# Row normalisation tile by tile in two attention sublayers, with its last step on ScalarE and the next rows turned in halves

## The chip, the cores and the metric

The kernel runs on one core of one Trainium2 chip. A core has five engines with queues of their own: TensorE (PE; its weight loads are shown as PEld), VectorE (DVE), ScalarE (ACT), GpSimd (POOL) and SyncE (SP), which issues the DMAs. They wait for each other by semaphores. The metric is the device time of one launch in microseconds; the kernel before takes 4338.36 us (median of three runs, 4335.82 to 4339.03).

## The reference

A decoder of four layers with three sublayers each, over 64 sequences of 64 tokens with 256 features, 4096 rows in all. After every sublayer the row is normalised:

```python
x = _layernorm(x + _L3_attn_ref(x, ...), axis=-1)     # tenth sublayer
x = _layernorm(x + _L3_xattn_ref(x, ctx_2048, ...), axis=-1)  # eleventh
x = _layernorm(x + _L3_ffn_ref(x, ...), axis=-1)      # twelfth
```

`_layernorm` takes the mean from the row and divides by the root of its variance plus 1e-5. The tenth is self-attention with 16 heads of 128, in which queries, keys and outputs are divided by their root mean square and a bias grows with the distance of two tokens. The eleventh attends to a context of 64 rows for each sequence, with 16 query heads and 4 key and value heads. The twelfth is a feed-forward layer with ternary weights. Both attentions are computed in 32-bit floats.

## The kernel before, in words

The 4096 rows lie in 8 groups of 512 rows; a group `X[g]` is one buffer of 128 partitions by 4 tiles by 256 features, and it stays on the chip from the first sublayer to the last. A tile is 128 rows, that is two sequences.

The tenth and eleventh sublayers run in one loop, `l3_attentions` (line 1787). A step is a group, a tile and a half `hb` of the 16 heads, so there are 64 steps for each sublayer. The loop is a software pipeline of depth four: in turn `i` of the loop, the queries and keys of step `i` are projected, step `i-1` has its queries and keys turned and its scores made, step `i-2` has its probabilities turned and its values summed, and step `i-3` has its outputs turned and projected. The 64 steps of the tenth are followed directly by those of the eleventh.

The order of the work: the loop stands in a region in which **TensorE** alone issues in the order in which the program emits its instructions. For the other engines a scheduler fixes the order when the program is built. It puts on an engine what its own reckoning takes to be ready, and among those what was emitted first. [...] A trace shows that order: the statistics of a group's tiles are all emitted with the fourth tile, yet those of the first three run right after their own additions.

Names and lines that matter below:

- `output` (lines 1977 and 2181): adds eight heads' share to the accumulator `acc`. With the second half of the heads it also makes `z[:, t]`, the sum of `acc` and `x` (lines 1991 and 2197, VectorE). With the fourth tile it calls `layernorm` (line 339) for the whole group.
- `layernorm`: `mean_rstd` (line 322) takes the statistics of each tile (lines 331 and 334, VectorE) and then calls `rsqrt` (line 300) once for the four tiles: an addition of epsilon on VectorE (line 303) and a power of -1/2 on GpSimd (line 305), on 128 by 4 numbers. Then line 342 applies mean and root to each of the four tiles, on VectorE.
- `normalized_parts` (line 350) is another form of the same, which other sublayers use: VectorE makes `nmr`, minus the mean times the root (line 361), and ScalarE applies both (line 363). In this loop it serves the ninth sublayer, whose groups are finished one ahead of the tenth (`linear.parts`, line 72): it makes xq (line 83), y (lines 94 to 96) and the normalised rows.
- `transposed` (line 314) turns a group's rows, eight transposes of 128 by 128 into two PSUM buffers, and copies each buffer to SBUF, as `xt`. In the eleventh sublayer `rows(g)` calls it at the end of the step of tile 3, `hb` 0, for the next group (line 2207), and once from the loop for group 0 (line 1853).
- `copy` (line 286) takes ScalarE and VectorE by turns, call by call (lines 290 and 292); it copies v, q, k, qT, pt, yt and xt. There are two PSUM buffers for transposes (`tr`), which qT, kT, pt, yt and xt share.
- The squares of y and of q and k are made by ScalarE at line 1884 and summed by VectorE at line 1885; the scores of the eleventh run on VectorE from line 2144 to 2151, with the exponential at 2149 on ScalarE and the division at 2152 on GpSimd.
- The twelfth sublayer's first rows are copied to SBUF by ScalarE at line 2297, and its first matmuls are at line 2306.

The buffer `z` is one of 128 by 4 by 256, used for a group at a time.

Of the kernel before, what the change touches and what calls it, by code (L numbers as in the profile page):

```python
# [10 lines left out]
F32 = mybir.dt.float32  # L11
# [3 lines left out]
AF = mybir.ActivationFunctionType  # L15
ALU = mybir.AluOpType
# [3 lines left out]
P = 128  # L20
D = 256
S = 64
TG = 4
NTOK = TG * P
# [246 lines left out]
class Decoder:  # L271
# [67 lines left out]
    def layernorm(self, out, z, eps=1e-5):  # L339
        mv, rstd = self.mean_rstd(z, TG, eps)  # L340
        for t in range(TG):
            self.nc.vector.tensor_scalar(
                out[:, t, :], z[:, t, :], mv[:, t, 0:1], rstd[:, t : t + 1], ALU.subtract, ALU.mult
            )

    def normalized(self, out, z):
        for part in self.normalized_parts(out, z):
            part()
# [1438 lines left out]
    def l3_attentions(self, ctx, linear):  # L1787

        wk = ctx.enter_context(self.tc.tile_pool(name="l3a", bufs=2, reuse_waits="tile"))
        steps = [(g, t, hb) for g in range(self.n_groups) for t in range(TG) for hb in range(2)]
        n = len(steps)
        none = lambda *a: None
        with self.tc.manual_schedule(engines={mybir.EngineType.PE}):
            one, two = self.l3_attn(wk, steps, linear), self.l3_xattn(wk, steps)
            row = [(one, i) for i in range(n)] + [(two, i) for i in range(n)]
            for i in range(2 * n + 3):
                at = lambda j: row[j] if 0 <= j < len(row) else (None, j)

                def do(stage, name, *a):
                    which, j = at(i - stage)
                    if which is not None:
                        getattr(which, name, none)(j, *a)

                turning = i == n
                do(0, "start")
                if i <= n:
                    do(2, "value")
                    do(1, "turn", 0)  # L1810
                    if not turning:
                        do(0, "query", 0)
                    do(1, "turn", 1)
                    if not turning:
                        do(0, "query", 1)
                    do(3, "outputs_turned")
                    do(0, "key", 0)
                    do(2, "turned")
                    do(1, "scores")
                    do(0, "key", 1)  # L1820
                    do(3, "output")
                    do(2, "values")
                    if turning:

                        two.load_biases()
                        do(0, "query", 0)
                        do(0, "query", 1)
                        do(0, "late")
                else:
                    do(2, "value")  # L1830
                    if i == n + 1:
                        two.load_output()
                    do(1, "turn", 0)
                    do(0, "query", 0)
                    do(1, "key_turned")
                    do(1, "turn", 1)


                    queries = i % 2 or i >= 2 * n or two.ready(i - n)
                    if not queries:  # L1840
                        do(0, "query", 1)
                    do(3, "outputs_turned")
                    do(3, "output")
                    do(1, "scores")
                    do(2, "turned")
                    if queries:
                        do(0, "query", 1)
                    if not i % 2:
                        do(0, "late")
                    do(2, "values")  # L1850
                do(0, "end")
                if i == n - 2:
                    two.rows(0)
                if i == n - 1:
                    two.load()

    def l3_attn(self, wk, steps, linear):
# [4 lines left out]
        nc = self.nc  # L1862
# [4 lines left out]
        nc.vector.tensor_scalar(both, kw, qw, 1.0 / math.sqrt(P), ALU.mult, ALU.mult)  # L1867
        half = lambda b: slice(b * S, (b + 1) * S)
        wide = lambda a, n: a.unsqueeze(2).broadcast_to([P, a.shape[1], n])
        xts, zs, state, accs = {}, {}, {}, {}  # L1870

        def projected(i, w, u, tag, bufs):
            g, t, hb = steps[i]
# [103 lines left out]
        def output(i):  # L1977
            g, t, hb = steps[i]
            yts = state.pop((i, "yt"))
            if hb == 0:  # L1980
                accs[g, t] = self.bank("acc", tag="acc", bufs=1)
            acc = accs[g, t]
            for h in range(8):
                n = 8 * hb + h
                nc.tensor.matmul(  # L1985
                    acc[:, :D], yts[h % 2][:, h // 2, :], wp[n // 8][:, (n % 8) * D : (n % 8 + 1) * D],
                    start=n == 0, stop=n == 15,
                )
            if hb == 1:
                x, z = self.X[g], zs[g]  # L1990
                nc.vector.tensor_tensor(z[:, t, :], acc[:, :D], x[:, t, :], ALU.add)
                if t == TG - 1:
                    self.layernorm(x, z)

        def start(i):
            g, t, hb = steps[i]
            if (t, hb) == (0, 0):
                if g + 1 < self.n_groups:
                    ahead[:] = linear.parts(g + 1, wk, bank)
                zs[g] = wk.tile([P, TG, D], F32, tag="z", name="z", bufs=1)  # L2000
            if g == 0 and hb == 0:
                ps = self.transpose4([self.X[0][:, t, c * P : (c + 1) * P] for c in range(2)], "xt")
                self.copy(xts[0][:, :, t * P : (t + 1) * P], ps[:, :D].rearrange("p (c n) -> p c n", c=2))

        def end(i):
# [13 lines left out]
        bias = self.distances(wk)  # L2019
        xts[0] = wk.tile([P, 2, NTOK], F32, tag="xt", name="xt")  # L2020
        return SimpleNamespace(
            start=start, value=value, turn=turn, query=query, outputs_turned=outputs_turned, key=key,
            turned=turned, scores=scores, output=output, values=values, end=end,
        )

    def l3_xattn(self, wk, steps):
# [4 lines left out]
        nc, ins = self.nc, self.ins  # L2031
# [23 lines left out]
            w.o = self.big_weight("l3x_wo")  # L2055

        half = lambda b: slice(b * S, (b + 1) * S)
        xts, zs, tiles, state, context = {}, {}, {}, {}, self.context

        def rms(x, out, name):  # L2060

# [5 lines left out]
        def ready(i):  # L2067
            return steps[i][:2] in context.tiles

        def loaded(i):  # L2070

            for k, name in enumerate("kv"):
                t = wk.tile([P, 4, P], F32, tag=name, name=name, bufs=2)
                self.load(t.rearrange("p h d -> p (h d)"), context.dram[(*steps[i][:2], k)])
                state[i, name] = t
# [105 lines left out]
        def output(i):  # L2181
            g, t, hb = steps[i]
            yts = state.pop((i, "yt"))
            if hb == 0:
                tiles[g, t, "acc"] = self.bank("acc", tag="acc", bufs=1)
            acc = tiles[g, t, "acc"]
            for h in range(8):
                n = 8 * hb + h
                nc.tensor.matmul(  # L2189
                    acc[:, :D], yts[h % 2][:, h // 2, :], w.o[n // 8][:, (n % 8) * D : (n % 8 + 1) * D],  # L2190
                    start=n == 0, stop=n == 15,
                )
            if hb == 1:
                if t == 0:
                    zs[g] = wk.tile([P, TG, D], F32, tag="z", name="z", bufs=1)
                x, z = self.X[g], zs[g]
                nc.vector.tensor_tensor(z[:, t, :], acc[:, :D], x[:, t, :], ALU.add)
                if t == TG - 1:
                    self.layernorm(x, z)

        def rows(g):
            xts[g] = self.transposed(self.X[g], wk, "xt")

        def end(i):
            g, t, hb = steps[i]
            if (t, hb) == (TG - 1, 0) and g + 1 < self.n_groups:
                rows(g + 1)
            if hb == 1 and i + 1 < len(steps) and ready(i + 1):
                loaded(i + 1)

            if len(steps) - i in (12, 8):
                ahead.extend(self.l3_prepare(len(self.l3_rows)))
            if ahead:
                ahead.pop(0)()

        ahead = []
        cs = lambda g, t: lambda c: self.CT[g][:, c, t * P : (t + 1) * P]
        return SimpleNamespace(
            load=load, load_biases=load_biases, load_output=load_output, rows=rows, turn=turn, query=query,
            late=late, ready=ready, key_turned=key_turned, turned=turned, scores=scores, output=output, values=values, end=end,  # L2220
        )

# [225 lines left out]
```

## Time and profile before

| what | value |
|---|---|
| median of three runs | 4338.36 us (4335.82 to 4339.03) |
| the profiled execution, its own time | 4343.85 us |
| its span | 4342.1 us |
| mean granted TensorE clock | 0.979 |
| tenth sublayer, about 1925 to 3195 us | 64 steps, some 20.0 us each |
| eleventh sublayer, about 3195 to 4042 us | 64 steps, some 12.6 us each after the handover |
| VectorE addition z, lines 1991 and 2197 | 64 times, 425 ns |
| VectorE statistics on z, line 331, in these two sublayers | 64 times, 427 ns |
| VectorE application, line 342, in these two sublayers | 64 times, 407 ns |
| ScalarE application, line 363, in the tenth sublayer's stretch | 28 times, 596 ns |
| GpSimd power, line 305, rstd of 128 by 4, in the tenth | 14 times, 1008 ns |
| GpSimd power, line 305, rstd of 128 by 1, in the twelfth | 64 times, 637 ns |

How to read the lines below. A line of a timeline has start and duration in microseconds, engine, line of the code, operation, what is written and read, how often it was merged, and in square brackets the idle time of the engine just before it, with what ended that. A line of waits names who waited, for whom, how long in all, how often, and the longest. PE, DVE, ACT and POOL are the engines as named above.

### The profile page before, as it was taken

What the parts mean: (1) busy time and instruction counts of PE and PEld (TensorE: products, weight loads), DVE (VectorE), ACT (ScalarE), POOL (GpSimd) and SP (SyncE); (2) the same over time, 40 slices, a digit from 0 to 9 for tenths busy, and PEclk for the clock granted to TensorE, in tenths of its full rate; (3) what the DMA queues carried; (4) which work ended last, traced back from release to release, by engine and by line L of the source; (5) the groups of instructions that cost most, each with busy time, mean ns of one, the idle gap of its engine ahead of it and who ended that gap; (6) DMA issues with size and microseconds to landing.
All of it is one profiled execution on the core that took longest, in us unless ns stands there. A gap on an engine that the chain in (4) does not pass through costs nothing. (4 is left out here: it accounts for less than half of the span.)

```text
span 4342.1 us, 74081 instructions
## 1 busy us (share of the span) xinstructions
PE 4079.0 (94%) x28788; PEld 2635.7 (61%) x28808; DVE 3092.6 (71%) x6211; ACT 2018.1 (46%) x3695; POOL 1498.3 (35%) x1529
## 2 busy tenths in 40 slices
PE   8889998989888999989999999999989999999898
PEld 5645566666665555546666666666656666666566
DVE  6844548888665687877777777777667777887676
ACT  5555535666523566544444444444432232332443
POOL 4411111332431111115555555555533444433111
PEclk9989999999999999999999999999999999999999
DMA  2200012333200000031111111111130000100000
GB/s 84 67 21 10 1 34 65 76 77 70 72 1 12 1 1 1 10 131 25 30 25 28 27 25 30 25 29 27 30 105 20 20 23 20 25 22 14 8 17 16
DMA packets 108296, 144.01 MB, mean 33 GB/s; under 512 B 15845, under 2 KB 73381, under 8 KB 106537
## 3 DMA queue, kind: packets, MB, share of 16 engines
q1 hardware_dynamic: 107944, 139.27, 12.6%
q8 instruction: 228, 3.74, 0.4%
q14 instruction: 124, 1.01, 0.1%
HBM read 70.25 MB, written 26.76 MB: 22 GB/s over the span
## 5 line engine op out<-in xcount | busy, mean ns | idle before, releaser
L305 POOL TENSOR_TENSOR hrq<-hrq,neg_half 128x4 f32<-128x4 f32 x256 | 258.5, 1010 | 573.9 <-DVE hrq L303 571.5
L305 POOL TENSOR_TENSOR rstd<-rstd,neg_half 128x4 f32<-128x4 f32 (+1 forms) x171 | 149.4, 875 | 705.5 <-DVE rstd L303 641.2
L1188 DVE TENSOR_REDUCE mc<-sq 128x2 f32<-128x512 f32 x512 | 317.3, 682 | 64.0 <-PE sk L1186 62.8
L1194 ACT ACTIVATE e<-sk 128x512 f32<-128x512 f32 x512 | 265.4, 606 | 114.0 <-PE sk L1186 111.6
L1183 PE MATMUL sq<-l1x 32*128 32x256 f32 x2048 | 277.2, 409 | 4.9 <-DVE z L1069 3.1
L1186 PE MATMUL sk<-l1x 32*128 32x256 f32 x2048 | 254.4, 394 | 0.2 <-DMA l1x<-l1x_m 0.2
L1703 PE MATMUL p<-l3a_wq,xt 128*128 128x512 f32 x512 | 242.1, 595 | 11.1 <-DVE v L292 9.9
L305 POOL TENSOR_TENSOR hrk<-hrk,neg_half 128x4 f32<-128x4 f32 x160 | 188.5, 1178 | 177.6 <-DVE hrk L303 173.0
L1703 PE MATMUL p<-l3a_wk,xt 128*128 128x512 f32 x512 | 247.4, 606 | 0.6 <-ACT q L290 0.6
L1183 PEld LDWEIGHTS sq<-l1x 32*128 32x128 f32 x2048 | 210.1, 195 | 57.8 <-issue 22.4
L1703 PE MATMUL p<-l3x_wq,xt 128*128 128x512 f32 x512 | 242.8, 597 | 0.7 <-DVE k L2087 0.7
L2189 PE MATMUL acc<-l3x_wo,yt 128*128 128x256 f32 x1024 | 239.7, 388 | 2.5 <-ACT yt L290 1.2
L1703 PE MATMUL p<-l3a_wv,xt 128*128 128x512 f32 x512 | 234.0, 599 | 0.4 <-ACT y L94 0.4
L1985 PE MATMUL acc<-l3a_wproj,yt 128*128 128x256 f32 x1024 | 232.0, 379 | 0.5 <-DVE yt L292 0.5
L1985 PEld LDWEIGHTS acc<-l3a_wproj,yt 128*128 128x128 f32 x1024 | 194.2, 190 | 53.7 <-issue 29.2
L2063 ACT ACTIVATE sq<-q 128x512 f32<-128x512 f32 x128 | 80.6, 630 | 314.0 <-DVE q L2087 306.7
L2189 PEld LDWEIGHTS acc<-l3x_wo,yt 128*128 128x128 f32 x1024 | 196.1, 195 | 36.7 <-issue 7.4
L311 PEld LDWEIGHTS qT<-ident,q 128*128 128x128 f32 x1024 | 122.1, 142 | 121.9 <-issue 79.8
L1186 PEld LDWEIGHTS sk<-l1x 32*128 32x128 f32 x2048 | 189.7, 188 | 6.9 <-issue 2.5
L311 PE MATMUL qT<-ident,q 128*128 128x128 f32 x1024 | 159.1, 278 | 26.8 <-DVE qT L292 19.6
L1969 POOL TENSOR_TENSOR hry<-hry,neg_half 128x8 f32<-128x8 f32 x64 | 106.3, 1660 | 183.3 <-DVE hry L1965 183.3
L1222 PE MATMUL ret<-e,vt 128*32 128x256 f32 x2048 | 139.2, 387 | 17.7 <-DVE mc L1188 16.9
(401 smaller groups left out, 10189.0 us busy)
## 6 DMA issues: line engine op xcount, KB each, us to landing
vs<-v SPq DMA_DIRECT2D x320, 128.0 KB
l3x_kv<-kv SPq DMA_DIRECT2D x28, 256.0 KB
x<-in_x SPq DMA_DIRECT2D x8, 512.0 KB
ct<-in_ctxT SPq DMA_DIRECT2D x8, 512.0 KB
cn<-in_ctx SPq DMA_DIRECT2D x8, 512.0 KB
l1x<-in_ctx SPq DMA_DIRECT2D x128, 32.0 KB
l1x_x<-x SPq DMA_DIRECT2D x8, 512.0 KB
l1x<-l1x_x SPq DMA_DIRECT2D x128, 32.0 KB
```

The costliest lines, as they stand in the source:

```text
L305: nc.gpsimd.tensor_tensor(out, out, self.neg_half[:, :n], ALU.pow)
L311: self.nc.tensor.transpose(ps[:, j * P : (j + 1) * P], blk, self.ident)
L1183: nc.tensor.matmul(ps[:, n, :], x_[rows, j, part], c_[rows, j, :], start=True, stop=True)
L1186: nc.tensor.matmul(ps[:, n, :], c_[rows, j, part], x_[rows, j, :], start=True, stop=True)
L1188: nc.vector.tensor_reduce(mc[new % 2][:, ra + k, 2 * j : 2 * j + 2], ps, AX.X, ALU.max, negate=True)
L1194: nc.scalar.activation(es[rb + k], ps, AF.Exp, scale=scale)
L1222: nc.tensor.matmul(ret[32 * r : 32 * r + 32, :], vt[i % 2][:, lc, 4 * r + j, :], es[r][:, lc, :], start=lc == 0, stop=lc == 1,)
L1703: self.nc.tensor.matmul(ps, lhs(c), w(c, cols), start=c == 0, stop=c == 1 and bias is None)
L1969: nc.gpsimd.tensor_tensor(r, r, self.neg_half[:, :8], ALU.pow)
L1985: nc.tensor.matmul(acc[:, :D], yts[h % 2][:, h // 2, :], wp[n // 8][:, (n % 8) * D : (n % 8 + 1) * D], start=n == 0, stop=n == 15,)
L2063: nc.scalar.activation(sq, x, AF.Square)
L2189: nc.tensor.matmul(acc[:, :D], yts[h % 2][:, h // 2, :], w.o[n // 8][:, (n % 8) * D : (n % 8 + 1) * D], start=n == 0, stop=n == 15,)
```

## The change

The function `tile_normalized` is new. It normalises one tile of 128 rows as soon as its sum is there: the addition, the statistics, the root for this tile alone, and then a function that makes `nmr` on VectorE and applies it on ScalarE, in place of line 342. Both sublayers' `output` call it for each tile and put the function on a list, and the loop runs the list after `end` of the same turn. The buffer `z` is now 128 by 256, two of them.

In the eleventh sublayer `rows` takes a half `c` of the features. The next group's rows are turned half by half: the first at the end of the step of tile 3 with `hb` 0, the second a step later. For group 0 the loop does it at two turns of the tenth sublayer in place of one. The tenth's own turning of rows is as before.

```diff
+    def tile_normalized(self, wk, x, a):
+        nc = self.nc
+        z = wk.tile([P, D], F32, tag="z", name="z", bufs=2)
+        st = self.smallp.tile([P, 6], F32, tag="bnst1", name="bnst1", bufs=4)
+        mv = self.smallp.tile([P, 2], F32, tag="bnmv1", name="bnmv1", bufs=4)
+        r, b = self.small(1, "rstd1", bufs=4), self.small(1, "nmr1", bufs=4)
+        nc.vector.tensor_tensor(z, a, x, ALU.add)
+        nc.vector.bn_stats(st, z)
+        nc.vector.bn_aggr(mv, st)
+        self.rsqrt(r, mv[:, 1:2], 1.0, 1e-5)
+
+        def apply():
+            nc.vector.scalar_tensor_tensor(b, mv[:, 0:1], -1.0, r, ALU.mult, ALU.mult)
+            nc.scalar.activation(x, z, AF.Identity, bias=b, scale=r)
+
+        return apply
...
+        self.row_ends = []
...
                 do(0, "end")
-                if i == n - 2:
-                    two.rows(0)
+                while self.row_ends:
+                    self.row_ends.pop(0)()
+                if i in (n - 3, n - 2):
+                    two.rows(0, i - n + 3)
...
             if hb == 1:
-                x, z = self.X[g], zs[g]
-                nc.vector.tensor_tensor(z[:, t, :], acc[:, :D], x[:, t, :], ALU.add)
-                if t == TG - 1:
-                    self.layernorm(x, z)
+                self.row_ends.append(self.tile_normalized(wk, self.X[g][:, t, :], acc[:, :D]))
...
-        def rows(g):
-            xts[g] = self.transposed(self.X[g], wk, "xt")
+        def rows(g, c):
+            if c == 0:
+                xts[g] = wk.tile([P, 2, NTOK], F32, tag="xt", name="xt")
+            ps = self.transpose4([self.X[g][:, t, c * P : (c + 1) * P] for t in range(TG)], "xt")
+            self.copy(xts[g][:, c, :], ps)
...
-            if (t, hb) == (TG - 1, 0) and g + 1 < self.n_groups:
-                rows(g + 1)
+            if t == TG - 1 and g + 1 < self.n_groups:
+                rows(g + 1, hb)
```

The third of these places stands for both `output` functions, which get the same edit.

More of the change, by code (lines that the diff above doesn't have):

```diff
@@ L1869, in l3_attn @@
         wide = lambda a, n: a.unsqueeze(2).broadcast_to([P, a.shape[1], n])
-        xts, zs, state, accs = {}, {}, {}, {}
+        xts, state, accs = {}, {}, {}
         def projected(i, w, u, tag, bufs):
@@ L1999, in start @@
                     ahead[:] = linear.parts(g + 1, wk, bank)
-                zs[g] = wk.tile([P, TG, D], F32, tag="z", name="z", bufs=1)
             if g == 0 and hb == 0:
@@ L2057, in l3_xattn @@
         half = lambda b: slice(b * S, (b + 1) * S)
-        xts, zs, tiles, state, context = {}, {}, {}, {}, self.context
+        xts, tiles, state, context = {}, {}, {}, self.context
         def rms(x, out, name):
@@ L2193, in output @@
             if hb == 1:
[L2194 to L2199, printed above, removed]
-        def rows(g):
-            xts[g] = self.transposed(self.X[g], wk, "xt")
+                self.row_ends.append(self.tile_normalized(wk, self.X[g][:, t, :], acc[:, :D]))
+        def rows(g, c):
[3 more added lines that the diff above has]
+            self.copy(xts[g][:, c, :], ps)
         def end(i):
             g, t, hb = steps[i]
-            if (t, hb) == (TG - 1, 0) and g + 1 < self.n_groups:
-                rows(g + 1)
+            if t == TG - 1 and g + 1 < self.n_groups:
+                rows(g + 1, hb)
             if hb == 1 and i + 1 < len(steps) and ready(i + 1):
```

## The prediction

> **What bounds the kernel now.** I read the page first, then the busy time by stretch, then TensorE's waits, then the timeline around the waits. From here on, "z+1.68" means 1.68 us after VectorE starts the addition z of a tile, so that tiles can be laid over each other.
>
> ```profile
> span 4342.1 us, 74081 instructions
> PE 4079.0 (94%) x28788; PEld 2635.7 (61%) x28808; DVE 3092.6 (71%) x6211; ACT 2018.1 (46%) x3695; POOL 1498.3 (35%) x1529
> ```
> ```profile
> core 0: us, PE busy (x) PEld busy (x) DVE busy (x) ACT busy (x) POOL busy (x), PEclk, DMA share, GB/s
> 1925.00:3195.00 1270.00, 1249.78 (x8541) 793.90 (x8542) 922.83 (x1805) 567.33 (x977) 673.18 (x584) 1.00 0.14 32
> 3260.00:4040.00 780.00, 748.10 (x5499) 518.28 (x5497) 596.39 (x1165) 232.27 (x412) 303.06 (x288) 0.99 0.08 20
> ```
>
> The first row is the tenth sublayer, the second the eleventh without the handover. TensorE is idle for 20 of 1270 us and for 32 of 780: no change of the row normalisation can be worth more than that and a little at the two ends. So the question is which of these idle microseconds end on an instruction that the change moves. TensorE's waits, one answer for each sublayer (total, times, longest):
>
> ```profile
> PE p L1703 <- DVE v L292: 9.9, 7, 1.4
> ```
> ```profile
> PE qT L311 <- DVE qT L292: 19.6, 11, 2.2
> PE qT L311 <- ACT xt L290: 6.5, 7, 1.0
> ```
>
> Seven times each: once for each group. The timeline shows the cause in the tenth sublayer, at the last tile of group 0:
>
> ```profile
> 2120.54 0.42 DVE L1991 TENSOR_TENSOR z<-acc,x 128x256 f32<-128x256 f32 x1 [0.38 <-PE acc L1985]
> 2121.67 0.17 DVE L303 TENSOR_SCALAR rstd<-bnmv 128x4 f32<-128x4 f32 x1
> 2121.92 1.01 POOL L305 TENSOR_TENSOR rstd<-rstd,neg_half 128x4 f32<-128x4 f32 x1 [0.35 <-DVE rstd L303]
> 2122.97 1.38 DVE L342 TENSOR_SCALAR x<-z,bnmv,rstd 128x256 f32<-128x256 f32 x4 [1.12 <-POOL rstd L305]
> 2124.26 0.68 DVE L1885 TENSOR_REDUCE hry<-sq 128x4 f32<-128x512 f32 x1
> 2127.06 0.68 DVE L292 COPY v<-p 128x512 f32<-128x512 f32 x1
> 2127.79 1.98 PE L1703 MATMUL p<-l3a_wq,xt 128*128 128x512 f32 x4 [1.41 <-DVE v L292]
> ```
>
> VectorE waits 1.12 us for GpSimd's power, then applies four tiles; L1885 starts at z+3.73, in the other tiles at z+1.68. The copy of v ends late and TensorE waits 1.41. In the eleventh sublayer the same block stands in front of the score chain:
>
> ```profile
> 3344.67 0.71 DVE L303 TENSOR_SCALAR rstd<-bnmv 128x4 f32<-128x4 f32 x1
> 3346.28 1.01 POOL L305 TENSOR_TENSOR rstd<-rstd,neg_half 128x4 f32<-128x4 f32 x1
> 3347.33 1.38 DVE L342 TENSOR_SCALAR x<-z,bnmv,rstd 128x256 f32<-128x256 f32 x4 [1.36 <-POOL rstd L305]
> 3348.63 0.68 DVE L2145 TENSOR_TENSOR s<-s,mask 128x512 f32<-128x512 f32 x1
> 3352.95 0.66 PE L311 MATMUL qT<-ident,q 128*128 128x128 f32 x4 [2.23 <-DVE qT L292]
> ```
>
> L2145 starts at z+5.10, elsewhere at z+1.89; the copy of qT is late and TensorE waits 2.23, in each of seven groups. The 0.9 us on xt is the turning of the next rows: eight transposes take both PSUM buffers, and the qT transposes behind them wait for a copy.
>
> **What the Trainium skill says.** "SBUF — State Buffer", Who interferes with whom: a VectorE tensor_scalar in a two-port mode and a GpSimd instruction exclude each other for the whole instruction. The trace agrees: L303 above takes 0.71 us instead of 0.17 and ends (3345.38) as GpSimd's 1.04 us product k ends (3345.35). The change adds L303s, so this counts. "Perfetto Trace Analysis", Tensor Engine Instruction: VectorE, ScalarE and GpSimd are strict first-in first-out. The trace agrees: ScalarE sat 1.70 us before an x at L363 that waited for nmr, with a ready square behind it. "ScalarE: Activation LUTs", Table sets: cheap functions are in every set. The trace agrees: L363 runs an Identity between exponentials in the tenth sublayer and no table load falls into either attention.
>
> **The change part by part.**
>
> *Removed.* 64 L342 on VectorE (0.41 us each, 1.38 for four) and 16 waits of 1.12 to 1.36 before them. If nothing took their place, TensorE's waits would go: 7 x 1.41 = 9.9 us and 7 x 2.23 = 15.6 us.
>
> *Added.* L303 and L305 once a tile instead of once a group: 48 more of each. The power on 128x1 takes 0.64 us in the last sublayer (row rstd 128x1, 637 ns), on 128x4 1.01; I take 0.64, with 1.01 as the upper end. An nmr of 0.16 us (as L361) on VectorE and an application of 0.59 us (as L363) on ScalarE per tile. ScalarE is 45% and 30% busy, GpSimd 53% and 39%; their busy time alone bounds nothing. What matters is where nmr stands on VectorE, since it waits for the power and everything behind it waits too. It is emitted at the end of the step, but only TensorE is in emission order. The statistics of tiles 0 to 2 are emitted with those of tile 3 and yet run right after their z; L361, emitted a step after its L303, stood next on VectorE and waited for the power in 7 of 7 cases. I therefore take it that **nmr is placed early and waits.**
>
> *Tenth sublayer.* L303 ends at z+1.31, the power runs z+1.39 to 2.03, nmr starts at z+2.07, L1885 at z+2.17 instead of 1.68: 0.5 late. The cover is the time from the end of the copy of v to the query matmul that reuses its buffer: 0.46, 0.75, 0.03 and 0.53 us at tiles 0 to 3 (tile 2 has the quantisation xq in the way, in six groups; the last from 1.41 against 2.05 late, less a semaphore's time). So only tile 2 pays: 6 x 0.5 = 3.0. With the power at 1.01 it is 0.87 late and a group pays 0.4 + 0.1 + 0.85 + 0.3 = 1.65, 13 in all. Sum: -9.9 + 3.0 = -6.9.
>
> *Eleventh sublayer.* Tiles 0 and 2: GpSimd is free, nmr slips in behind the score product L2144 at z+2.07, L2145 0.3 late against a cover of 0.24 (qT copy to the next transposes): 0.06. Tile 3: L303 stalls 0.6 behind the product k; the power queues behind the one for hrq and ends at z+3.39 instead of 3.76; L2145 at z+3.5 instead of 5.10, so 2.23 becomes about 0.65. Tile 1 is in the same place, newly 1.6 late; but the halved turning flips the alternation of copies for a step, and that qT copy goes to ScalarE; the half's copy stays exposed: 0 to 1.5, I take 0.7. A group pays 0.06 + 0.65 + 0.06 + 0.7 = 1.5; 7.5 groups make 11. Sum: -15.6 + 11 = -4.6.
>
> *Turning in halves.* Four transposes and one copy at each of two steps: the second buffer is free for qT, 7 waits of about 0.9 go: -6.5. The copy of the first half has a whole step, that of the second has the qT transposes and the key projection (1.9 us) ahead of its first use: nothing. If the copy is taken up late behind VectorE's block, up to 0.9 comes back, which is in tile 1's bound. No DMA moves; SP's queue is untouched.
>
> *The end.* The last sublayer's first matmul waited 3.84 us at 4043.20, because ScalarE's copy of its rows waited for the last L342 (4042.3). The new application ends near z+2.9 = 4041.4: -1.0. Bounds: 0, and -3.4 if that copy's buffer no longer lies on z.
>
> Sum: -6.9 - 4.6 - 6.5 - 1.0 = -19. Against its own time, the profiled execution would go from 4343.85 (span 4342.1) to 4325; it lies 5.5 above the median 4338.36, which goes to **4319**.
>
> **Rivals.** *All of it is gained.* If nmr is placed behind other ready work, no power is waited for; tile 3's L303 stall (0.6) is below its cover (0.87), and a microsecond or two remains: -9.5 - 14.5 - 6.5 - 1.0 = -31.5, 4307. For it: nmr is emitted last. Against: L361.
>
> *The wait is moved, not removed* (the change then doesn't do what it says). The power on 128x1 takes 1.01 here too, and tile 1 pays in full: tenth -9.9 + 13 = +3; eleventh, tiles 0 and 2 0.37 each, tile 3 1.03, tile 1 1.5, 3.3 x 8 = 26, so +11; turning -6.5, end -0.5: +7, 4345. For it: 64 waits replace 16.
>
> *ScalarE's queue becomes the bound: slower.* If the application is placed ahead of the squares of y (L1884, now z+1.05) in the tenth sublayer, they start near z+2.9 and L1885 is 1.8 late: 1.34 + 1.05 + 1.77 + 1.27 = 5.4 a group, 43 in all instead of 3. With the other terms: -19 + 40 = +21, 4359. It decides from about 16 tiles of 32 (1.35 each against the 22 gained elsewhere), and is slower by over 0.2% from 23. For it: the 1.70 us at L363. Against: the squares are emitted first and ready first.
>
> **How the numbers follow.** 0.2%, 8.7 us, is about what a measurement of this kernel can tell from no change. Chances: forecast 0.40 (own range 4311 to 4329), all gained 0.20, moved 0.20, ScalarE 0.20. Faster is the first two, 0.60; within 0.2% the third, 0.20; slower the fourth, 0.20. The range runs from 4305 to 4347 and leaves out the fourth.
>
> **What would show it.** TensorE's waits of 1.41 and 2.23 gone, waits of at most 0.7 at tiles 1 and 3 of the eleventh sublayer; L305 rstd on 128x1 at 0.64; nmr with a wait on the power before it in most tiles; no qT wait on xt; L1884 still at z+1.05. Wrong if nmr never waits (then 4307), if L1884 or the copies pt and v wait behind the application, or if the order shifts elsewhere and new waits come up in tiles without a stall now.

## The result, and the profile after

The change made the kernel slower by a little: 4350.00 us (median of 13 runs, 4342.91 to 4354.92) against 4342.66 us for the kernel before in the same session (13 runs). The ratio is 1.0017, with a 95% interval of 1.0010 to 1.0025. The profiled execution has a span of 4346.2 us against 4342.1, at a clock of 0.982 against 0.979. The forecast was 4319.

Lines of the new code, as they appear below: L353 to L355 are the addition z and its statistics, L303 and L305 epsilon and the power as before, L359 is nmr, L360 the application on ScalarE. L1721 is the projection (it was L1703), L1905 and L1906 are the squares of y and their sum (L1884, L1885), L2161 to L2169 the score chain of the eleventh (L2144 to L2152).

The page's first lines, after:

```profile
span 4346.2 us, 74064 instructions
PE 4078.6 (94%) x28788; PEld 2630.0 (61%) x28808; DVE 3080.2 (71%) x6259; ACT 2053.0 (47%) x3759; POOL 1515.8 (35%) x1577
```

VectorE lost 12 us of work and ScalarE gained 35, as the change says. TensorE's busy time is the same over the whole span, so its waits come first. The same two stretches as before, after the change:

```profile
core 0: us, PE busy (x) PEld busy (x) DVE busy (x) ACT busy (x) POOL busy (x), PEclk, DMA share, GB/s
1925.00:3195.00 1270.00, 1238.06 (x8385) 781.88 (x8386) 909.26 (x1809) 575.24 (x997) 676.43 (x603) 1.00 0.13 30
3260.00:4040.00 780.00, 748.86 (x5552) 516.52 (x5551) 599.91 (x1212) 255.68 (x450) 316.82 (x316) 1.00 0.09 22
```

In the tenth sublayer TensorE now idles 32 us of 1270 instead of 20, with 156 fewer matmuls done in the stretch; in the eleventh it idles 31 of 780, as before. TensorE's waits after the change:

```profile
PE qT L311 <- DVE qT L292: 20.9, 12, 3.0
PE p L1721 <- DVE v L292: 10.2, 10, 1.4
PE p L1721 <- ACT y L94: 7.0, 7, 1.1
PE kT L311 <- ACT qT L290: 5.7, 7, 1.0
PE kT L311 <- DVE xq L83: 4.4, 6, 0.7
PE qT L311 <- DVE xt L292: 1.6, 7, 0.2
```

The wait on the copy of v is as large as before (9.9 then), but comes at other tiles, and three larger waits are new: on y (L94), on xq (L83) and on the qT copy of ScalarE (L290). The 6.5 us on xt have become 1.6. A tenth-sublayer tile of the changed kernel, tile 0 of group 1, shows why:

```profile
2164.58 0.42 DVE L353 TENSOR_TENSOR z<-acc,x 128x256 f32<-128x256 f32 x1 [0.38 <-PE acc L2006]
2165.95 0.56 POOL L305 TENSOR_TENSOR rstd<-rstd,neg_half 128x1 f32<-128x1 f32 x1 [0.33 <-DVE rstd L303]
2166.54 0.16 DVE L359 SCALAR_TENSOR_TENSOR nmr<-bnmv,rstd 128x1 f32<-128x1 f32 x1 [0.67 <-POOL rstd L305]
2166.74 0.60 ACT L360 ACTIVATE x<-z,nmr,rstd 128x256 f32<-128x256 f32 x1 [3.58 <-DVE nmr L359]
2167.24 1.06 ACT L1905 ACTIVATE sq<-y 128x512 f32<-128x512 f32 x2
2167.85 0.69 DVE L1906 TENSOR_REDUCE hry<-sq 128x4 f32<-128x512 f32 x1 [1.15 <-ACT sq L1905]
2170.32 0.68 DVE L292 COPY v<-p 128x512 f32<-128x512 f32 x1
2171.05 1.98 PE L1721 MATMUL p<-l3a_wq,xt 128*128 128x512 f32 x4 [0.97 <-DVE v L292]
```

ScalarE is idle for 3.58 us, and its next instruction is the application, which waits for nmr. Behind it stand the squares of y, whose inputs are there since about 2165.6 (before the change they started at z+1.05). They start at z+2.66 now. VectorE loses 0.67 us before nmr and another 1.15 before L1906; the copy of v is late and TensorE waits 0.97 us. In the trace the application stands ahead of the squares in 30 of the first 31 tiles of this sublayer. This is the prediction's third rival, at a lower price, and one of the signs that it named for being wrong.

The change of +7.3 us in the medians is also, almost to the microsecond, the sum of the second rival (+7). That is chance: that rival rests on a power of 1.01 us, and the trace shows 0.56.

### The profile page after: what moved, and what is told of

Read it like the earlier page. It is cut to its first block, busy times and chain, and to the rows that moved or that the text cites. A ratio compares the mean times of both kernels' runs of the same rounds, so it can differ in the third digit from the quotient of the medians.

```text
span 4346.2 us, 74064 instructions
## 1 busy us (share of the span) xinstructions
PE 4078.6 (94%) x28788; PEld 2630.0 (61%) x28808; DVE 3080.2 (71%) x6259; ACT 2053.0 (47%) x3759; POOL 1515.8 (35%) x1577
## 3 DMA queue, kind: packets, MB, share of 16 engines
q8 instruction: 228, 3.74, 0.4%
## 4 chain that ended last, share of the span: by engine, by line
PE 59%; DVE 19%; POOL 6%; ACT 5%; issue 4%; DMA 0%; SPq 0%; ACTq 0%; POOLq 0%; DVEq 0%
PE p L1721 15%; PE acc L2006 5%; PE acc L2206 4%; PE sq L1201 3%; POOL rstd L305 2%; PE ret L1240 2%; PE gate L1542 2%; PE up L1542 2%; DVE bnst L331 2%; PE acc L1558 2%; PE gate L904 2%; PE qT L311 2%; DVE mc L1206 2%; PE sk L1204 2%; PE up L904 2%
## 5 line engine op out<-in xcount | busy, mean ns | idle before, releaser
L305 POOL TENSOR_TENSOR rstd<-rstd,neg_half 128x1 f32<-128x1 f32 (+1 forms) x219 | 168.4, 769 | 729.8 <-DVE rstd L303 664.7
L305 POOL TENSOR_TENSOR hrq<-hrq,neg_half 128x4 f32<-128x4 f32 x256 | 258.5, 1010 | 459.5 <-DVE hrq L303 447.9
L1721 PE MATMUL p<-l3a_wq,xt 128*128 128x512 f32 x512 | 242.7, 597 | 12.5 <-DVE v L292 10.2
L305 POOL TENSOR_TENSOR hrk<-hrk,neg_half 128x4 f32<-128x4 f32 x160 | 188.1, 1176 | 183.8 <-DVE hrk L303 180.3
L1721 PE MATMUL p<-l3a_wk,xt 128*128 128x512 f32 x512 | 247.4, 606 | 0.5 <-ACT q L290 0.5
L1721 PE MATMUL p<-l3a_wv,xt 128*128 128x512 f32 x512 | 235.6, 601 | 7.0 <-ACT y L94 7.0
L1721 PE MATMUL p<-l3x_wq,xt 128*128 128x512 f32 x512 | 241.0, 593 | 1.2 <-DVE k L2104 1.2
L2206 PEld LDWEIGHTS acc<-l3x_wo,yt 128*128 128x128 f32 x1024 | 191.9, 191 | 34.6 <-issue 7.6
```

Source lines behind the costliest of these rows:

```text
L305: nc.gpsimd.tensor_tensor(out, out, self.neg_half[:, :n], ALU.pow)
L1721: self.nc.tensor.matmul(ps, lhs(c), w(c, cols), start=c == 0, stop=c == 1 and bias is None)
L2206: nc.tensor.matmul(acc[:, :D], yts[h % 2][:, h // 2, :], w.o[n // 8][:, (n % 8) * D : (n % 8 + 1) * D], start=n == 0, stop=n == 15,)
```

## The experiments

The times are medians. For comparing parts, the traces are cut at the starts of the additions z, numbered 0 to 63 (0 to 31 are the tenth sublayer's tiles, 32 to 63 the eleventh's): "tenth" is z0 to z28, "handover" z31 to z32, "eleventh" z32 to z60. The stretch ahead of the tenth took 1918 to 1927 us in all these executions, and the change doesn't touch it; the totals carry this scatter. A stretch is from one execution, the profiled one. Two short stretches stand in no column: z28 to z31 takes 119.2 us before, 124.2 after and 119.5 to 122.6 in the other kernels; z60 to z63 takes 63.5 before and 61.6 after. From z0 to z63 the changed kernel is 6.6 us longer than the kernel before.

| kernel | us | ratio to before (95%) | tenth | handover | eleventh |
|---|---|---|---|---|---|
| before | 4342.66 | 1 | 1117.0 | 33.7 | 702.2 |
| after | 4350.00 | 1.0017 (1.0010 to 1.0025) | 1131.0 | 25.8 | 699.6 |
| tenth_only | 4348.91 | 1.0013 (1.0004 to 1.0021) | 1131.0 | 25.3 | 700.7 |
| eleventh_norm_only | 4350.60 | 1.0025 (1.0016 to 1.0034) | 1116.9 | 33.5 | 711.6 |
| halves_only | 4330.39 | 0.9975 (0.9965 to 0.9984) | 1117.0 | 34.6 | 692.7 |
| squares_first | 4326.55 | 0.9962 (0.9948 to 0.9976) | 1106.9 | 26.1 | 699.6 |
| early_on_vector | 4333.82 | 0.9980 (0.9971 to 0.9989) | 1112.1 | 31.9 | 698.9 |
| both_late | 4297.41 | 0.9897 (0.9883 to 0.9910) | 1103.1 | 26.0 | 677.8 |
| late_on_vector | 4298.27 | 0.9902 (0.9889 to 0.9916) | 1103.6 | 25.2 | 680.2 |
| late_old_buffers | 4297.00 | 0.9898 (0.9884 to 0.9911) | 1103.3 | 25.7 | 677.4 |
| late_whole_rows | 4305.95 | 0.9923 (0.9910 to 0.9937) | 1103.1 | 25.5 | 689.8 |

**squares_first** changes one place in the changed kernel: in the tenth sublayer the application is issued on ScalarE behind the last square of y of that step (`behind_act`).

```diff
-            nc.scalar.activation(x, z, AF.Identity, bias=b, scale=r)
+            if self.behind_act is None:
+                nc.scalar.activation(x, z, AF.Identity, bias=b, scale=r)
+            else:
+                with self.tc.issue_after(self.behind_act):
+                    nc.scalar.activation(x, z, AF.Identity, bias=b, scale=r)
...
```

> The changed kernel with one order fixed: in the tenth sublayer ScalarE's application x stands behind the squares of y in ScalarE's queue. Nothing is left out. If ScalarE's queue is what costs the tenth sublayer, the first sum of squares goes from z+3.27 back to about z+2.1, the waits of 0.97, 0.73 and 1.10 us at tiles 0, 2 and 3 shrink to under 0.5, and the time falls by 12 to 18 us against the changed kernel, to 0.2 or 0.3% below the kernel before. If the wait for the power on VectorE is what costs, the waits stay above 0.6 and the time stays within 5 us of the changed kernel.

The same place of a tile in squares_first, tile 0 of group 1:

```profile
2156.83 1.08 ACT L1910 ACTIVATE sq<-y 128x512 f32<-128x512 f32 x2 [2.48 <-PE y L1980]
2157.74 0.16 DVE L359 SCALAR_TENSOR_TENSOR nmr<-bnmv,rstd 128x1 f32<-128x1 f32 x1 [0.67 <-POOL rstd L305]
2157.82 0.68 DVE L1911 TENSOR_REDUCE hry<-sq 128x4 f32<-128x512 f32 x1
2157.94 0.60 ACT L364 ACTIVATE x<-z,nmr,rstd 128x256 f32<-128x256 f32 x1
2161.12 1.88 PE L1725 MATMUL p<-l3a_wq,xt 128*128 128x512 f32 x4
```

With z at 2155.78 the squares are back at z+1.05; nmr still waits 0.67 us, and the query matmuls wait for nothing. The tenth shrinks by 24.1 us (1131.0 to 1106.9), more than expected: 18.4 of them are idle time (24.84 to 6.47), and 5.7 are busy time of TensorE, at a granted clock of 1.00 in both. A wait costs more than its idle time: the four matmuls take 1.98 us above and 1.88 here, and in a stream without a wait the first of them starts before the end of the transposes ahead. The next transposes start at z+8.29 in the changed kernel and at z+7.06 here, 1.23 us apart for a wait of 0.97. The place in ScalarE's queue is shown to be the cause in the tenth sublayer.

**tenth_only** has the change in the tenth sublayer alone (one buffer z and fewer of the small ones, the eleventh as before).

> The change in the tenth sublayer alone; the eleventh normalises and turns as before, and there is one buffer z in place of two. Nothing is left out. If the loss lies in the tenth, this is slower than the changed kernel: +12 to +20 us on the kernel before, 0.3 to 0.45%. If it lies in the eleventh, the time is that of the kernel before or less.

The tenth takes 1131.0 us, as in the changed kernel. The total is a miss, 5.5 us above the kernel before where 12 to 20 were expected, because the handover is 8.4 us shorter, which the expectation left out. So the loss and the handover's gain both belong to the tenth's part.

**halves_only** is the kernel before with the eleventh's next rows turned in halves and nothing else.

> The kernel before with the next rows of the eleventh sublayer turned in halves, the normalisation as before. Nothing is left out. If the halves are good by themselves, the seven waits of 0.9 us on xt go and nothing comes in their place: -6 us, 0.15%. If the swapped alternation of copies is what brings the new waits of kT on qT (0.7 to 1.0 and 0.24 us in the changed kernel), these appear here too and the time is within 2 us of the kernel before.

The seven waits on xt are gone and nothing took their place: the eleventh is 9.5 us shorter, where 6 were expected. Alone, this part makes the kernel faster.

**eleventh_norm_only** has the new normalisation in the eleventh sublayer, rows turned whole, the tenth as before, and the old buffer z of four tiles.

> The new normalisation in the eleventh sublayer alone: the tenth and the whole rows of the eleventh as before the change. Theory (nmr's early wait of 1.35 us for the power in the odd tiles holds VectorE, delays the scores' softmax chain and the copies, and eats what the halves gain): the wait of the transposes in tile 1 for xt stays at about 0.9 us per group, and nmr adds waits of its own there; the stretch from z 32 to z 60 is 706 to 711 us against 702.2 before, the time 0.1 to 0.2% above before (4346 to 4352 us). Rival (the new steps and the halves get into each other's way only together): the new steps alone take some 4 us from tile 3 and add nothing, 697 to 702 us, and the time is 0.1 to 0.2% under before.

Its waits:

```profile
PE qT L311 <- DVE qT L292: 18.2, 12, 2.1
PE qT L311 <- ACT xt L290: 16.8, 7, 2.5
```

The theory held, and went further than expected: the wait on xt grew from 6.5 to 16.8 us. The changed kernel's tile 1 of group 0 shows the start of it:

```profile
3309.24 0.42 DVE L353 TENSOR_TENSOR z<-acc,x 128x256 f32<-128x256 f32 x1 [0.16 <-PE acc L2206]
3309.94 1.04 POOL L2119 TENSOR_TENSOR k<-k,hrk 128x512 f32<-128x512 f32 x1
3310.38 0.15 DVE L303 TENSOR_SCALAR rstd<-bnmv 128x1 f32<-128x1 f32 x1
3310.94 1.01 POOL L305 TENSOR_TENSOR hrq<-hrq,neg_half 128x4 f32<-128x4 f32 x1
3311.92 0.55 POOL L305 TENSOR_TENSOR rstd<-rstd,neg_half 128x1 f32<-128x1 f32 x1
3312.50 0.16 DVE L359 SCALAR_TENSOR_TENSOR nmr<-bnmv,rstd 128x1 f32<-128x1 f32 x1 [1.35 <-POOL rstd L305]
3312.58 0.68 DVE L2162 TENSOR_TENSOR s<-s,mask 128x512 f32<-128x512 f32 x1
```

The power of this tile queues on GpSimd behind the product k and the power of hrq; VectorE stands 1.35 us at nmr, and the mask starts at z+3.34. Before, in tile 1, that was z+1.89. So this new wait stands in tile 1 as well as in tile 3, and whatever VectorE and ScalarE copy for TensorE in tile 1 is 1.4 us later: with whole rows xt, on which the qT transposes depend; with halves ScalarE's copy of qT and VectorE's of xt.

**both_late** takes the changed kernel and puts nmr behind the last copy of y in the tenth and behind the scores' subtraction in the eleventh (VectorE), and the application behind the squares or the exponential (ScalarE).

```diff
-            nc.vector.scalar_tensor_tensor(b, mv[:, 0:1], -1.0, r, ALU.mult, ALU.mult)
-            nc.scalar.activation(x, z, AF.Identity, bias=b, scale=r)
+            with self.tc.issue_after(self.behind_dve):
+                nc.vector.scalar_tensor_tensor(b, mv[:, 0:1], -1.0, r, ALU.mult, ALU.mult)
+            with self.tc.issue_after(self.behind_act):
+                nc.scalar.activation(x, z, AF.Identity, bias=b, scale=r)
...
```

> The changed kernel with both orders fixed in both sublayers: nmr behind the last copy of y (tenth) or the subtraction of the maximum (eleventh) on VectorE, the application behind the squares of y or the exponential on ScalarE. Nothing is left out. If early places in the queues are the whole of it, nmr never waits for the power, the tenth has no wait over 0.3 us that the kernel before has not, the 1.6 us at tile 3 of the eleventh goes below 0.3, and the time is 0.5 to 0.7% below the kernel before (-22 to -31 us). If the additional instructions themselves cost it, the gain is under 0.2%.

Its waits on qT:

```profile
PE qT L311 <- DVE qT L292: 9.3, 12, 1.9
```

It beats both kernels by about 1%, more than expected; nmr stands idle for the power in at most two of the 64 tiles. In the eleventh, 21.8 us go against the changed kernel: the mask starts at z+1.94 in every tile (within 0.01), the waits of tile 3 fall from 1.6 to 0.25 us, and those in tile 1 on ScalarE's qT copy go altogether. They came from nmr's early wait, then, and not from the halves. This run moves two instructions at once. In the tenth squares_first parts them: the application's place is worth 24.1 us, nmr's another 3.8 (1106.9 to 1103.1).

**late_on_vector** is both_late with the last step as one `tensor_scalar` of 128x256 on VectorE at nmr's late place. **early_on_vector** is the changed kernel with that same step on VectorE, its place left to the scheduler. The edit shown is that of early_on_vector; in late_on_vector the new line stands inside `issue_after(self.behind_dve)`.

```diff
-            nc.vector.scalar_tensor_tensor(b, mv[:, 0:1], -1.0, r, ALU.mult, ALU.mult)
-            nc.scalar.activation(x, z, AF.Identity, bias=b, scale=r)
+            nc.vector.tensor_scalar(x, z, mv[:, 0:1], r, ALU.subtract, ALU.mult)
```

> Both late, but the last step is one tensor_scalar of 128x256 on VectorE at nmr's late place (0.41 us by the trace of the kernel before) in place of nmr (0.16 us) there and the application (0.60 us) on ScalarE. Theory (where the step stands in its queue decides, and not which engine does it): within 0.15% of both_late, 4291 to 4304 us. Rival (what pays is that VectorE is freed of the last step): VectorE has 0.25 us more to do in each tile ahead of a copy that TensorE waits for, up to 16 us in 64 tiles, so 4305 to 4315 us.

> The changed kernel with its order as it is (the last step free to start as soon as the power is done), but as one tensor_scalar on VectorE in place of nmr and the application on ScalarE. Theory (in the tenth sublayer it is the place in ScalarE's queue, ahead of the squares, that costs): the squares start near z+1.05 again, the stretch from z 0 to z 28 is 1107 to 1116 us (squares_first 1106.9; VectorE's block is 0.25 us longer) against 1131.0; the eleventh keeps the early wait for the power and stays at 698 to 708 us; total 4325 to 4338 us. Rival (the early wait of VectorE for the power is what costs in both): the tenth stays above 1125 us and the total at 4345 us or more.

With the changed kernel and both_late these two make a square of engine and place. Late, the totals don't tell the engines apart (4297.41 and 4298.27 us); the eleventh is 2.4 us shorter with ScalarE (677.8 against 680.2). Early, the step costs the tenth 18.9 us more on ScalarE (1131.0 against 1112.1), where it stands ahead of the squares, and next to nothing more in the eleventh (699.6 against 698.9), where VectorE waits for the power in both; the handover is 6.1 us shorter on ScalarE, for a reason given below under "Not in the sum". Both theories held. With nothing of the step on ScalarE, the place on VectorE alone is worth 18.7 us in the eleventh (698.9 early, 680.2 late). That the last step was taken off VectorE, the change's own idea, is worth little beside that, and nothing that the late totals can tell.

**late_whole_rows** is both_late with the rows turned whole.

> Both late, with the eleventh's next rows turned whole as before the change. Theory (the halves are worth the 9.5 to 12 us that they gave with the old and with the early normalisation, because the eight transposes take both buffers whatever the normalisation does): the waits on xt are back at 0.9 us or more in 7 groups, the stretch from z 32 to z 60 is 687 to 690 us against 677.8, total 4307 to 4310 us. Rival (with the normalisation late there is slack that hides the whole rows): the stretch at 677 to 681 us, total 4297 to 4301 us.

The eleventh takes 12.0 us more than in both_late, with 10.1 us of waits on xt in 7 groups. The halves are worth 9.5 us with the old normalisation (halves_only), 12.0 with the early new one (711.6 to 699.6) and 12.0 with the late one. The expected stretch was met; the total is a microsecond under what was expected.

**late_old_buffers** is both_late with the small buffers of the statistics shared with the twelfth's preparation of rows, as before the change.

```diff
-        st = self.smallp.tile([P, 6], F32, tag="bnst1", name="bnst1", bufs=4)
+        st = self.smallp.tile([P, 1, 6], F32, tag="bnst", name="bnst", bufs=4)[:, 0, :]
...
-        r, b = self.small(1, "rstd1", bufs=4), self.small(1, "nmr1", bufs=4)
+        r, b = self.small(1, "rstd", bufs=4), self.small(1, "nmr", bufs=4)
```

> Both late, and in addition the eleventh's and tenth's statistics, powers and nmr use the four rotating buffers that the twelfth's preparation of rows uses (as the layer normalisation did before the change). Theory (the new waits at tile 0 of groups 1 and 2 of the eleventh, 1.80 and 1.89 us, come from the twelfth's preparation, which now runs some 400 us earlier because nothing holds its buffers back): the preparation's statistics go back to about the last two groups, these two waits fall to the 1.2 to 1.3 us of the other groups or go, and the stretch from z 32 to z 60 is 1 to 4 us shorter than 677.8 us; total 4293 to 4297 us, 0 to 0.1% under both_late. Rival (the waits belong to the rows turned in halves and have nothing to do with the preparation): the preparation moves, the waits stay at 1.8 to 1.9 us and the stretch at 677 to 679 us.

Half a miss. With buffers of its own for the new statistics, the twelfth's preparation ran early (its first application at 3329.7 us in both_late, 3370.1 in the changed kernel); with shared ones it is back at 3840.9 (3857.4 before), and the waits of 1.80 and 1.89 us in groups 1 and 2 are gone. But tile 3 waits 3.74 us in all instead of 1.76, tile 1 1.73 instead of nothing, and the stretch is the same (1 to 4 us less were expected). The early preparation is a side effect of the change, shown, and costs nothing on balance.

## Why the prediction was wrong

**The bound** was read rightly in kind: what moved are TensorE's waits. As a limit it is a little loose, because a wait also costs some of TensorE's busy time. From before to after the tenth lost 14.0 us, 9.4 of it idle and 4.6 busy time.

**Tenth sublayer, -6.9.** The step that failed is the placing of the application, "Against: the squares are emitted first and ready first". In the built program it stands ahead of the squares nearly everywhere, and the tenth became 14.0 us longer. The rest of that paragraph was right in kind: with the squares first, the tenth is 10.1 us shorter than before, nmr waits 0.67 us in nearly every tile, L1911 is some 0.4 us late where 0.5 was forecast, and only tile 2 pays (0.15 us on xq in four groups).

One reading under it was wrong. Before the change L1885 starts at z+1.68 in tile 0, but at z+2.23 in tile 1, behind the copy of xt, and at z+2.29 in tile 2 of six groups; the prediction took 1.68 for all. This made the third rival's price too high, though its mechanism was right: 5.4 us a group were foreseen, and TensorE waits 0.97, 0.14, 0.73 and 1.10 at tiles 0 to 3, 2.9 in all; squares_first puts the whole price at 24.1 / 7 = 3.4. The terms off most are tile 1 (1.05 foreseen, 0.14 measured) and tile 2 (1.77 and 0.73). With L1906 now at z+3.27 in every tile, tile 0 is 1.59 us late, but tiles 1 and 2 only 1.04 and 0.98, not 1.8. In tile 1 the copy of v ends at z+6.42 instead of 5.36, and the query matmuls were due at z+6.17, so that little is left to wait for. At tile 3 the wait is on ScalarE's y (L94) and not on the copy of v.

The line of the Trainium skill ("Perfetto Trace Analysis", Tensor Engine Instruction: VectorE, ScalarE and GpSimd are strict first-in first-out) was cited, and this case's trace agrees once more: ScalarE is idle for 3.58 us with ready squares behind. What failed was guessing the order, not the rule. Why the scheduler took this order isn't shown by a trace.

**nmr early and waiting** was right: nmr waits for the power noticeably in 47 of 64 tiles, 43.9 us on VectorE in all. The power on 128x1 took 0.56 us, against 0.64 taken.

**Eleventh sublayer, -4.6.** Its sign was wrong. Alone (eleventh_norm_only) the normalisation made the stretch 9.4 us longer. Two terms failed. Tile 3: the mask starts at z+3.34, where z+3.5 was foreseen, yet TensorE still waits 1.6 instead of 0.65. In group 3 the copy of qT starts at z+8.68 before and z+8.03 after, so of the 1.76 us at the mask only 0.65 arrive: from mask to copy VectorE takes 4.69 us instead of 3.58, mainly since the sum of the exponentials and the reciprocal, which stood behind the copy, now stand ahead of it. The step assumed the old order. Tile 1: 0 to 1.5 us were allowed and 0.7 taken; it is 1.05 a group in the changed kernel (5.70 and 1.65 over seven groups), and with whole rows the wait on xt rose by 1.5. Tile 0 of group 0, foreseen at nothing, waits 3.00: there the power queues behind two of hrq's, and nmr waits 2.74.

**Turning in halves, -6.5.** Right in mechanism, too small in size: 9.5 us alone. The seven waits are 6.5; the eleventh's idle time fell by 7.8 (27.2 to 19.4), and the rest is again busy time, at a granted clock of 0.99 in both. In the changed kernel the halves are worth 12.0 us (711.6 without them, 699.6 with them), but the normalisation has cost 9.4 of that.

**The end, -1.0.** The wait of the twelfth's first matmul fell from 3.84 to 2.58: -1.3.

**Not in the sum:** the handover, 7.9 us shorter. It hangs on a piece of the twelfth's preparation that the change doesn't mean to touch. Before the change, TensorE waits 5.61 us here for probabilities of the eleventh:

```profile
3248.77 0.41 POOL L2231 PARTITION_ALL_REDUCE tgam<-tcol  x1 [7.34 <-DVE tcol L2230]
3249.74 0.19 DVE L2151 RECIPROCAL smx<-smx 128x8 f32<-128x8 f32 x1
3256.21 1.03 POOL L2152 TENSOR_TENSOR s<-s,smx 128x512 f32<-128x512 f32 x1 [7.04 <-DVE smx L2150]
3257.30 1.11 PE L311 MATMUL pt<-ident,s 128*128 128x128 f32 x4 [5.61 <-POOL s L2152]
```

The product s on GpSimd, which makes the probabilities, starts 6.3 us after its last input, the reciprocal, is done. It is not VectorE that holds it, though the profile names VectorE: ahead of it in GpSimd's queue stands a sum over all partitions of the twelfth's weights, recorded with 0.41 us, and in all eleven kernels GpSimd starts nothing for 7 to 8 us after such a sum starts. In before, halves_only, eleventh_norm_only and early_on_vector this sum stands ahead of the product, TensorE waits 5.61, 5.96, 5.40 and 3.34 us, and the handover takes 31.9 to 34.6 us. In the other seven it does not fall there, no such wait comes, and the handover takes 25.2 to 26.1. In tenth_only the product starts at 3254.47 and the sum at 3261.86. The order on VectorE goes with it: before, the 2.27 us reduction that feeds this sum ran ahead of the exponentials' sum (3246.36 and 3248.55), in tenth_only behind it (3254.77 and 3252.91). No run moves the sum over the partitions alone.

Nor was the granted clock of TensorE in the sum. Before the change it falls to half for 3.4 us at four of the seven waits of 2.23 us in the eleventh, in the changed kernel once, at a wait of 2.09; its mean there is 0.990 and 0.998. At the wait of 2.23 us shown in the prediction, for example, it is 0.51 from 3354.2 to 3357.6. If half of each 3.4 us of work is lost, an estimate from these figures is 6.8 us before and 1.7 after. TensorE's idle time in the eleventh rose by 1.1 us (27.2 to 28.3) and its busy time fell by 3.7: the 2.6 us that the eleventh gained are the clock's by this estimate, not the waits'. In eleventh_norm_only there are five such drops, so that of the 12.0 us that the halves gave from there, some 6.8 are the clock's too.

Of the rivals, "all of it is gained" named the cure: with nmr placed behind other ready work it foresaw -31.5, and both_late measures a ratio of 0.9897, some 45 us. In its trace the rest lies in the handover (7.7 us), the tenth (13.9 where 9.5 was foreseen) and the eleventh (24.4 where nmr and the halves made 21.0).

## What to carry to other kernels

Before pricing an added instruction, find its neighbours in the queue of its own engine, and price both places, ahead of the ready work and behind it: here the place of a 0.16 us and a 0.60 us instruction was worth about 1% of the kernel, and with the late place the engine nothing that the totals tell. A small step that waits for another engine belongs behind work that is ready anyway, and an ordering constraint is the way to put it there when a scheduler decides. When a block ahead of a chain gets shorter, check that the order behind it stays, or else count only what reaches the copy that TensorE waits for. And where the instruction that a wait is put down to was done long before, look at what stands ahead in the queue of the engine that is late.

## What the runs showed of the hardware

- L303 on 128x4 took 0.71 us beside GpSimd's product k in the kernel before. On 128x1 it took 0.15 us with the same product running (3310.38, above), in all 15 such tiles of the eleventh. The Trainium skill, "SBUF — State Buffer", Who interferes with whom, says that a tensor_scalar can enter a two-port mode when its operands meet the conditions; with one element per partition it was not held back here. The prediction's 0.6 us stall in tile 3 didn't come.
- The power on GpSimd took 0.56 us on 128x1 and 1.01 on 128x4.
- A matmul behind a wait costs more than the wait: four took 1.98 us after a wait, 1.88 without, and what followed them came 1.23 us later for a wait of 0.97.
- A PARTITION_ALL_REDUCE on GpSimd is recorded with about 0.4 to 0.8 us, but GpSimd's next instruction started 7.1 to 8.2 us after its start, in each of the 22 cases around the handover in eleven traces.
- Long waits of TensorE went with half the granted clock, for 3.4 us or twice that, beginning in the wait or up to 3.5 us behind it. Between z0 and z60 of the eleven traces this shows at none of 75 waits of 1.0 to 1.5 us, at 3 of 35 of 1.5 to 1.8, and at 41 of 65 longer ones.
